# Products of the identity with itself in TensorE's waits between the last ranks and the first layer's first product

## The chip, the cores and the metric

The kernel runs on one core of one Trainium2 chip. The time is device microseconds from one launch; "before" is the median of three runs. One more execution was profiled, and all views of engines, waits and clock come from that execution. The engines are TensorE (PE; its weight loads are PEld), VectorE (DVE), ScalarE (ACT), GpSimd (POOL) and SyncE (SP, which here only issues DMAs). "Granted clock" is the share of TensorE's full clock that the throttle let through.

## The reference

4096 tokens of 512 numbers are rotated by a quaternion product, routed to two of eight experts each with a capacity of 1024 slots per expert, passed through the expert's two layers, weighted and added to the input.

```python
def reference(x, cond_256, q_right, spectral_gate, gate_w, fc1_w, fc1_b, fc2_w, fc2_b):
    xr = hamilton(normalize(cond_256), hamilton(x * spectral_gate, conj(normalize(q_right))))
    xf = xr.reshape(4096, 512)
    scores = softmax(xf @ gate_w.T)                  # 8 experts
    topv, topi = top_k(scores, 2)
    gates = topv / topv.sum(-1, keepdims=True)
    # place of each (token, choice) in its expert: all first choices, then all second choices
    loc = running_count_per_expert(topi)             # valid while loc < 1024
    de = scatter(xf, topi * 1024 + loc)              # (8, 1024, 512)
    h = relu(de @ fc1_w.T + fc1_b)                   # (8, 1024, 2048)
    eo = h @ fc2_w + fc2_b                           # (8, 1024, 512)
    return x + sum_over_choices(eo[slot] * gates * valid)
```

The filter in the reference (a transform, a gain for each channel, the inverse transform) is a gain for each channel. Everything is f32.

## The kernel before, in words

The kernel has two parts. The first is the routing, inside a block that ends at line 535. The 4096 tokens are taken in two groups of 16 tiles of 128 tokens (`GROUPS`, `last` is 1). For each group `logits` (line 328) multiplies the tokens by the rotated gate, `turned` and `choose` find the two experts on VectorE and build running counts `cnt`, `rank` (line 387) sums the counts over the partitions on TensorE, and `places` turns ranks into a tile number and a lane for each token's slot. `one_hots` (lines 428 to 433) builds f16 arrays W and A on VectorE for half a group (8 tiles of tokens, 16 pairs of token and choice). `tokens` (line 444) is 16 products of A's and W's slices, 128x64 each, that add up in one PSUM bank `tok_ps`: after four calls the bank holds which token sits in which slot.

The order in which the engines get their instructions is the order of the program text (`manual_schedule`), each engine taking its own in turn. Around the change it is: ranks of the last group, one_hots and tokens of the first group's second half (0,1), a few tensor operations on POOL that find which slots are taken, places and then one_hots and tokens of the last group's halves (last,0) and (last,1); the A of the very last half is built in two parts of eight pairs (`parts=2`). VectorE then makes `slot_tok`, `tokf` and `slot_add` (lines 501 to 506); four f32 products (line 510) spread tokf into `quarter_ps`, which line 525 turns into the gather indices `quarter` of later experts; lines 529 to 535 make `slot_cho`.

`lt_ps` are the two PSUM banks of the logits, read for the last time by `turned`. `ident` is a 128x128 f32 identity, made by POOL near the start and used for transposes.

The second part is the experts. `first_layers` begins by gathering the first expert's eight rows of 128 slots from x (POOL, line 560, indices slot_tok), and `rotated(0)` transposes the first four rows on TensorE (line 687, four 128x128 transposes a row, one for each quarter j, into four banks `xps`), then applies the rotation: ScalarE writes the j = 0 share of output quarter i (line 695), VectorE adds j = 1, 2, 3 (line 697). The result is `xa`. Four f32 products for each i (line 833 in `layer1_plain`, tile `p`, two blocks and two halves m; eight MATMUL instructions) make the first quarter of the first expert's first layer. `rotated(1)` does the same for the other four rows (tiles `xc`, `xb`) after three of the four i groups have been issued. From the second quarter on, layers run in the seven-product form (`layer1`, line 722, and the second layers, line 735), for 8 experts of 4 quarters each, and a generator pair interleaves first and second layers on TensorE. POOL computes sums of blocks for them (lines 124 to 139) and gathers the next expert's rows (`xq`, line 637).

PSUM after line 535 is divided into `ps_x` (one bank), `ps_1` (two buffers of two banks, tag p1: the first layer's accumulators) and `ps_2` (three banks). Buffers of a tag are handed out in turn.

Of the kernel before, what the change touches and what calls it, by code (L numbers as in the profile page):

```python
# [28 lines left out]
F32 = mybir.dt.float32  # L29
# [8 lines left out]
P = 128  # L38
# [9 lines left out]
HALF = 512  # L48
PER = HALF // P
# [15 lines left out]
def kernel(  # L65
# [12 lines left out]
    nc = tc.nc  # L78
# [16 lines left out]
    ident = const.tile([P, P], F32, name="ident")  # L95
# [4 lines left out]
    slot_add = const.tile([P, NS], I32, name="slot_add")  # L100
    slot_cho = const.tile([P, NS], I32, name="slot_cho")
    quarter = const.tile([P, NS, QT], I32, name="quarter")

    def load_w1(k):
        e, g = divmod(k, NG)
        w = wpool.tile([P, 2, 2, 2, HB], F32, tag="w1", name=f"w1_{k}")
        nc.sync.dma_start(w, w1[e, g])
        return w

    def load_w2(k):  # L110
        e, g = divmod(k, NG)
        w = wpool.tile([P, 2, 2, D], F32, tag="w2", name=f"w2_{k}")
        nc.sync.dma_start(
            w, w2[e, g * HG : (g + 1) * HG, :].rearrange("(a c p) d -> p a c d", p=P, c=2)
        )
        return w
# [14 lines left out]
    def left1(k, w):  # L131

        s = [wsum.tile([P, 2, HB], F32, tag=f"s{i}", name=f"s{i}_{k}") for i in range(4)]
        G = nc.gpsimd
        steps = [
            lambda: G.tensor_tensor(s[0], w[:, 1, 0], w[:, 1, 1], ALU.add),  # L136
            lambda: G.tensor_tensor(s[1], s[0], w[:, 0, 0], ALU.subtract),
            lambda: G.tensor_tensor(s[2], w[:, 0, 0], w[:, 1, 0], ALU.subtract),
            lambda: G.tensor_tensor(s[3], w[:, 0, 1], s[1], ALU.subtract),  # L139
        ]  # L140
        return [w[:, 0, 0], w[:, 0, 1], s[3], w[:, 1, 1], s[0], s[1], s[2]], steps

    def right2(k, w):

        return sums(
            wsum,
            "t",
            k,
            [P, 2, DB],
            w[:, 0, :, :DB],  # L150
            w[:, 0, :, DB:],
            w[:, 1, :, :DB],
            w[:, 1, :, DB:],
            minus=True,
        )
# [10 lines left out]
    with ExitStack() as rctx:  # L166
# [8 lines left out]
        def bank(pool, tag, n=""):  # L175
            return pool.tile([P, 512], F32, tag=tag, name=f"{tag}{n}")
# [145 lines left out]
        lt_ps = [bank(rps, "lt", g) for g in range(GROUPS)]  # L322
# [95 lines left out]
        def one_hots(g, c, hi, lo, parts=1):  # L418

            hi, lo = (  # L420
                a[:, c * TC : (c + 1) * TC].rearrange("p t k -> p (t k)") for a in (hi, lo)
            )
            tok = tok_no[:, g * TG + c * TC : g * TG + (c + 1) * TC].rearrange("p t k -> p (t k)")
            of_tile = [P, NS, TC * K]
            B = oh.tile(of_tile, F16, tag="B", name=f"B{g}_{c}")
            W[g, c] = oh.tile(of_tile, F16, tag="W", name=f"W{g}_{c}")
            A[g, c] = oh.tile([P, P, TC * K], F16, tag="A", name=f"A{g}_{c}")
            V.tensor_tensor(B, tile_no, hi.unsqueeze(1).to_broadcast(of_tile), ALU.is_equal)
            V.tensor_tensor(W[g, c], B, tok.unsqueeze(1).to_broadcast(of_tile), ALU.mult)
            n = TC * K // parts  # L430
            for i in range(parts):
                part = slice(i * n, (i + 1) * n)
                V.tensor_tensor(
                    A[g, c][:, :, part],
                    lane[:, :, part],
                    lo[:, part].unsqueeze(1).to_broadcast([P, P, n]),
                    ALU.is_equal,
                )

        def tokens(g, c):  # L440

            for t in range(TC):
                for k in range(K):
                    nc.tensor.matmul(  # L444
                        tok_ps[:, k, :],
                        lhsT=A[g, c][:, :, t * K + k],
                        rhs=W[g, c][:, :, t * K + k],
                        start=g == 0 and c == 0 and t == 0 and k == 0,
                        stop=g == GROUPS - 1 and c == TG // TC - 1 and t == TC - 1,
                        skip_group_check=True,  # L450
                    )
# [16 lines left out]
        rank(last)  # L468
        one_hots(0, 1, *at)
        tokens(0, 1)  # L470


        SE = [P, E, PT]
# [18 lines left out]
        at = places(last)  # L492
        one_hots(last, 0, *at)
        tokens(last, 0)
        one_hots(last, 1, *at, parts=2)
        tokens(last, 1)


        has0, not0, any_ = (a.rearrange("p e s -> p (e s)") for a in (has0, not0, any_))
# [9 lines left out]
        for c in range(QT):  # L509
            nc.tensor.matmul(  # L510
                quarter_ps[:, c],
                lhsT=spread[:, c].rearrange("p q w -> p (q w)"),
                rhs=tokf,
                start=True,
                stop=True,
            )


        den = rp.tile([P, NT], F32, name="den")
# [8 lines left out]
        t = rp.tile([P, NS], F32, name="t")  # L528
# [20 lines left out]
    ps_1 = ctx.enter_context(tc.tile_pool(name="ps_1", bufs=2, space=PSUM))  # L549
# [304 lines left out]
    def first_layers():  # L854

        xs = Slots(0)
        xs.gather(0)
        xs.gather(1)
        load_b2(0)

        def rotated(half):

            t = [xs.bank(half, j, *((ps_x, "xps") if j == 3 else (ps_2, "p2"))) for j in range(NJ)]
            for st in range(PER):
                for j in range(NJ):
                    xs.transpose(half, j, st, t[j])
            for i in range(NJ):
                for j in range(NJ):
                    xs.add(half, i, j, t[j])

        rotated(0)
        xf, fill = xs.factors()
        left_f, w1_t, w2_t = None, None, None
        nxt = None
        for k in range(NK):
            e, g = divmod(k, NG)
            if k + 1 < NK:
                w1_t, w2_t = load_w1(k + 1), load_w2(k + 1)
                left_n, steps = left1(k + 1, w1_t)
                loaded[k + 1] = w2_t  # L880
            else:
                left_n, steps = None, []
            if g == 0 and e + 1 < E:
                nxt = Slots(e + 1)
            if g == NG - 1 and e + 1 < E:
                xf_n, fill_n = nxt.factors()
                steps = [f for pair in zip(steps, fill_n) for f in pair]
                per = 2
            else:
                per = 1  # L890
            if k == 0:
                rights[0], more = right2(0, w2_next)
                for f in [*more, *steps]:
                    f()
                steps = []
            units = layer1(k, (left_f, xf)) if k else layer1_plain(k, w1_next, xs)
            for i, _ in enumerate(units):
                if k == 0 and i == 2:
                    rotated(1)
                    for f in fill:  # L900
                        f()
                if k == 0 and i == 1:
                    nc.scalar.dma_start(choice.rearrange("(p t) c -> p t c", p=P), picked)

                    nc.scalar.dma_start(*(a.rearrange("(b r) d -> r b d", r=PT) for a in (out, x)))
                if e + 1 < E:

                    if (g, i) in ((0, 12 if e else 5), (1, 6)):
                        fetches.extend(nxt.quarters(g))
                    if (g, i) in ((1, 9), (2, 5)):  # L910
                        background.extend(nxt.steps(g - 1))

                if i in (7, 8, 9, 13):
                    assert per == 1 or nxt.rotated == 2 * NJ
                    for f in steps[:per]:
                        f()
                    steps = steps[per:]
                yield
            left_f = left_n
            if g == NG - 1 and e + 1 < E:  # L920
                xf = xf_n
# [6 lines left out]
    def load_b2(e):  # L928
        b2_sb = op.tile([P, D], F32, tag="b2", name=f"b2_{e}")
        nc.gpsimd.dma_start(b2_sb, b2[e : e + 1, :].to_broadcast([P, D]))  # L930
        biases[e] = b2_sb.unsqueeze(1).to_broadcast([P, 4, D])
# [138 lines left out]
```

## Time and profile before

| what | us |
|---|---|
| runs before: lowest, median, highest | 1649.4, 1653.91, 1654.48 |
| the profiled execution, its time | 1635.26 |
| its span, first to last instruction | 1633.5 |
| mean granted clock of TensorE over the span | 0.988 |
| TensorE's wait for the logits' weights, at the start | 6.2 |
| TensorE's waits for VectorE's A (three) | 5.7 |
| TensorE's waits for the first expert's rows (three) | 2.6 |
| TensorE's wait for xa ahead of the first layer's first product | 2.7 |

The table's waits are TensorE's idle time ahead of an instruction, by what released it. A block in the timeline stands as start, length, engine, line, operation, output and inputs, shape and count; its length runs from the first start to the last modelled end, so the last instruction's pass through the array is in it. A window row gives each engine's busy time in that stretch and, after them, the granted clock. The first eight MATMULs of the logits take 1.94 us, the fifth such block 1.59 us and the sixth 1.06 us; in the trace the granted clock reads 1.00 until its first recorded change.

### The profile page before, as it was taken

The page shows a single profiled execution, that of the slowest core. Times are in us where ns is not written, and L with a number is a line of the kernel's source. Part 1 is how long each engine was busy: PE and PEld are TensorE (multiplying, and loading weights), DVE is VectorE, ACT ScalarE, POOL GpSimd, SP SyncE. Part 2 cuts the span into 40 slices and gives each one's busy share as a digit, 9 for nine tenths or more (in the row PEclk, how much of TensorE's full clock was granted, in tenths as well). Part 3 has the DMA queues.
Part 4 walks back from the last instruction along what each step waited for, and adds up shares of the span by engine and source line. Part 5 has one row for each costly group of instructions (what it writes and reads, how often), then busy time and mean ns, then how long its engine had stood idle before and what let it go on. Part 6 is the DMA issues. An engine that isn't in the chain of part 4 may idle for free.

```text
span 1633.5 us, 14524 instructions
## 1 busy us (share of the span) xinstructions
PE 1582.3 (97%) x5558; PEld 1039.0 (64%) x5558; DVE 912.3 (56%) x1291; ACT 284.5 (17%) x393; POOL 897.0 (55%) x747
## 2 busy tenths in 40 slices
PE   4899999999999999999999999999999999999996
PEld 1456666666666666666666666666666666666665
DVE  7537744575455754577345774457644575454335
ACT  1122111221112211122111211121111221111110
POOL 1576255862668445784367735586266844544304
PEclk8799999999999999999999999999999999999999
DMA  7542103311222113320133210331122311230003
GB/s 311 176 147 72 52 5 139 110 64 52 96 75 92 54 52 110 116 74 17 52 127 114 75 52 1 140 112 66 52 81 72 105 55 52 104 108 30 23 26 102
DMA packets 47998, 137.31 MB, mean 84 GB/s; under 512 B 9334, under 2 KB 9590, under 8 KB 42808
## 3 DMA queue, kind: packets, MB, share of 16 engines
q1 hardware_dynamic: 22800, 75.54, 12.5%
q0 software_dynamic: 20736, 52.32, 9.7%
q10 hardware_dynamic: 4392, 8.52, 1.4%
q8 instruction: 44, 0.72, 0.2%
q14 instruction: 26, 0.21, 0.0%
HBM read 119.77 MB, written 25.23 MB: 89 GB/s over the span
## 4 chain that ended last, share of the span: by engine, by line
PE 91%; DVE 2%; issue 2%; ACT 2%; DMA 2%; POOL 1%; SPq 0%; POOLq 0%; DVEq 0%; ACTq 0%
PE a L735 26%; PE a L722 25%; PE b L722 20%; PE b L735 18%; PE p L833 2%; ACT xa L695 1%; DMA xb<-in_xt_dram 1%; DVE xps L652 1%; DMA rows<-out_dram,slot_tok 0%; POOL rows L560 0%; POOL out_dram L606 0%; ACT u L766 0%; PE tok_ps L444 0%; ACT h L766 0%; DMA rows<-in_x_dram,slot_tok 0%
## 5 line engine op out<-in xcount | busy, mean ns | idle before, releaser
L766 ACT ACTIVATE u<-a,b_sb 128x512 f32<-128x512 f32 x186 | 127.9, 687 | 851.7 <-PE a L722 851.7
L637 POOL DMA_INDIRECT xq<-in_xq_dram,quarter x224 | 231.2, 1032 | 62.0 <-issue 58.4
L735 PEld LDWEIGHTS a<-t,hs 128*128 128x128 f32 x1024 | 194.6, 190 | 79.4 <-issue 59.3
L735 PE MATMUL a<-t,hs 128*128 128x256 f32 x1024 | 241.9, 379 | 0.0
L722 PE MATMUL a<-x,s 128*128 128x512 f32 x496 | 233.1, 592 | 0.0
L136 POOL TENSOR_TENSOR s<-w 128x512 f32<-128x512 f32 x31 | 39.3, 1268 | 224.2 <-PE b L722 224.1
L139 POOL TENSOR_TENSOR s<-w,s 128x512 f32<-128x512 f32 x31 | 39.7, 1279 | 204.1 <-PE b L722 204.0
L722 PEld LDWEIGHTS a<-x,s 128*128 128x128 f32 x496 | 94.2, 190 | 65.7 <-issue 59.3
L722 PE MATMUL a<-x,w 128*128 128x512 f32 x248 | 117.3, 595 | 9.7 <-ACT h L766 9.7
L735 PEld LDWEIGHTS b<-w,h 128*128 128x128 f32 x512 | 97.2, 190 | 42.1 <-issue 20.6
L735 PE MATMUL b<-w,h 128*128 128x256 f32 x512 | 121.1, 379 | 2.1 <-DVE acc L996 2.1
L735 PEld LDWEIGHTS a<-t,h 128*128 128x128 f32 x512 | 97.1, 190 | 40.5 <-issue 25.1
L735 PEld LDWEIGHTS a<-w,h 128*128 128x128 f32 x512 | 97.3, 190 | 39.7 <-issue 29.7
L735 PEld LDWEIGHTS b<-t,hs 128*128 128x128 f32 x512 | 97.3, 190 | 39.7 <-issue 26.5
L735 PEld LDWEIGHTS b<-w,hs 128*128 128x128 f32 x512 | 97.3, 190 | 39.3 <-issue 28.9
L735 PE MATMUL a<-t,h 128*128 128x256 f32 x512 | 121.1, 379 | 0.8 <-DVE v L983 0.8
L735 PE MATMUL b<-t,hs 128*128 128x256 f32 x512 | 121.0, 379 | 0.0
L735 PE MATMUL a<-w,h 128*128 128x256 f32 x512 | 121.0, 379 | 0.0
L735 PE MATMUL b<-w,hs 128*128 128x256 f32 x512 | 120.9, 379 | 0.0
L722 PE MATMUL a<-xa,w 128*128 128x512 f32 x248 | 116.6, 592 | 0.8 <-ACT u L766 0.8
L722 PE MATMUL b<-xa,w 128*128 128x512 f32 x248 | 116.5, 592 | 0.0
L722 PE MATMUL b<-x,s 128*128 128x512 f32 x248 | 116.5, 592 | 0.0
(169 smaller groups left out, 2143.3 us busy)
## 6 DMA issues: line engine op xcount, KB each, us to landing
w<-in_w_dram SPq DMA_DIRECT2D x64, 1024.0 KB, 7.8
xb<-in_xt_dram SPq DMA_DIRECT2D x8, 1024.0 KB, 11.2
out_dram<-in_x_dram ACTq DMA_DIRECT2D x1, 8192.0 KB
xq<-in_xq_dram,quarter POOLq DMA_INDIRECT x224, 2.5
b<-in_b_dram POOLq DMA_DIRECT2D x8, 256.0 KB, 3.6
c<-choice,slot_cho POOLq DMA_INDIRECT x64, 3.1
rows<-out_dram,slot_tok POOLq DMA_INDIRECT x64, 5.8
out_dram<-rows,slot_add POOLq DMA_INDIRECT x64, 2.8
```

The source lines that it names most:

```text
L136: lambda: G.tensor_tensor(s[0], w[:, 1, 0], w[:, 1, 1], ALU.add),
L139: lambda: G.tensor_tensor(s[3], w[:, 0, 1], s[1], ALU.subtract),
L637: nc.gpsimd.indirect_dma_start(out=self.xg[half][st][:, q * P : (q + 1) * P], out_offset=None, in_=xq, in_offset=bass.IndirectOffsetOnAxis ...
L652: V.transpose(t[:, st * P : (st + 1) * P].rearrange("p (q w) -> p q w", w=CW), self.xg[half][st].rearrange("p (q j w) -> p j q w", q=QT, j ...
L695: nc.scalar.activation(to, t, AF.Copy, scale=M[:, i, 0:1])
L722: nc.tensor.matmul(out[:, m], lhsT=factors[0][n][:, c, m * P : (m + 1) * P], rhs=factors[1][n][:, c, :], start=first and c == 0, stop=c == ...
L735: nc.tensor.matmul(out[:, m], lhsT=factors[0][n][:, c, (st0 + m) * P : (st0 + m + 1) * P], rhs=factors[1][n][:, c, :], start=first and m = ...
L766: nc.scalar.activation(to[:, m], a[:, m], func, bias=bias[:, m : m + 1])
L833: nc.tensor.matmul(ps[n][:, m], lhsT=w[:, block, i // 2, i % 2, m * P : (m + 1) * P], rhs=x.of(half, i), start=i == 0, stop=i == NJ - 1,)
```

## The change

A helper `idle(t, n)` issues n products of `ident` with `ident` into the first 128 columns of a PSUM tile; nobody reads the result. It is called with 5 after tokens(0,1), 5 after tokens(last,0), 6 after tokens(last,1) and 10 after the line 510 products, all into `lt_ps[0]`. In `rotated(0)` it is called with 3 after each of the first three rows' transposes and 12 after the fourth, into a `spare` tile that is taken from `ps_1` (tag p1) ahead of the first layer's own tiles. That is 47 products. `rotated(1)` has none.

```diff
+    def idle(t, n):
+
+        for _ in range(n):
+            nc.tensor.matmul(t[:, :P], lhsT=ident, rhs=ident, start=True, stop=True)
@@
         one_hots(0, 1, *at)
         tokens(0, 1)
+        idle(lt_ps[0], 5)
@@
         one_hots(last, 0, *at)
         tokens(last, 0)
+        idle(lt_ps[0], 5)
         one_hots(last, 1, *at, parts=2)
         tokens(last, 1)
+        idle(lt_ps[0], 6)
@@
                 start=True,
                 stop=True,
             )
+
+        idle(lt_ps[0], 10)
@@
             t = [xs.bank(half, j, *((ps_x, "xps") if j == 3 else (ps_2, "p2"))) for j in range(NJ)]
+            spare = ps_1.tile([P, 2, HALF], F32, tag="p1", name="spare")[:, 0] if half == 0 else None
             for st in range(PER):
                 for j in range(NJ):
                     xs.transpose(half, j, st, t[j])
+                if half == 0:
+                    idle(spare, 3 if st + 1 < PER else 12)
```

## The prediction

> **What bounds the kernel now.** I read the page first, for the engine that sets the span and for the clock granted to it.
>
> ```profile
> span 1633.5 us, 14524 instructions
> PE 1582.3 (97%) x5558; PEld 1039.0 (64%) x5558; DVE 912.3 (56%) x1291; ACT 284.5 (17%) x393; POOL 897.0 (55%) x747
> PEclk8799999999999999999999999999999999999999
> ```
>
> The reader sees TensorE busy 97% of the span and a granted clock that is down only in the first slices (40.8 us each). All the change touches lies there, so I read the chain of waits over the first 120 us (start, length, what).
>
> ```profile
> 38.03 1.15 DVE A L433
> ...
> 39.23 4.21 PE tok_ps L444 x32
> ...
> 44.44 1.25 POOL rows L560
> ...
> 47.26 3.92 DMA rows<-in_x_dram,slot_tok
> ...
> 51.23 1.34 PE xps L687 x5
> ...
> 52.64 0.70 ACT xa L695
> ...
> 55.89 13.49 PE p L833 x24
> 69.38 1.75 PE xps L687 x16
> 71.12 17.34 PE p L833 x40
> ```
>
> The chain runs through the last tokens products, the POOL row gathers, the third row's landing, transposes, ScalarE and VectorE (three adds of 0.76 us), and from 55.89 TensorE itself. The same p products cost 17.34/40 = 0.434 us at the end and 13.49/24 = 0.562 us at the start: 24 at 0.434 would be 10.40, so 3.09 us are lost. Then TensorE's timeline, with the idle time before each block in brackets, shows where fills can go.
>
> ```profile
> 26.75 2.22 PE L444 MATMUL tok_ps<-W,A 128*128 128x64 f16 x16 [1.87 <-DVE A L433]
> 35.12 2.19 PE L444 MATMUL tok_ps<-W,A 128*128 128x64 f16 x16 [1.93 <-DVE A L433]
> 39.23 4.20 PE L444 MATMUL tok_ps<-W,A 128*128 128x64 f16 x32 [1.91 <-DVE A L433]
> 44.43 1.94 PE L510 MATMUL rank<-tokf,spread 128*128 128x64 f32 x8 [1.00 <-DVE tokf L505]
> 51.23 1.97 PE L687 MATMUL xps<-ident,rows 128*128 128x128 f32 x8 [0.48 <-DMA rows<-in_x_dram,slot_tok]
> 69.21 1.91 PE L687 MATMUL xps<-ident,rows 128*128 128x128 f32 x16
> ```
>
> Last, busy time by 2 us windows (length, then PE, PEld, DVE, ACT and POOL busy with instruction counts, granted clock, DMA share, GB/s) dates the clock.
>
> ```profile
> 26.00:28.00 2.00, 1.25 (x10) 1.26 (x11) 1.90 (x5) 0.01 (x1) 0.00 (x0) 0.92 1.07 399
> 28.00:30.00 2.00, 0.96 (x8) 0.80 (x7) 1.73 (x6) 0.31 (x1) 0.00 (x0) 0.50 1.03 419
> 60.00:62.00 2.00, 2.00 (x4) 0.76 (x3) 1.93 (x4) 0.00 (x0) 1.92 (x3) 0.55 0.43 108
> 62.00:64.00 2.00, 2.00 (x6) 0.87 (x5) 0.53 (x1) 0.00 (x0) 2.00 (x3) 1.00 0.52 199
> ```
>
> The clock falls to half in the first row (0.92 is full for 84%: at 27.7) and rises in the third (0.55: 10%, at 61.8), 5.9 us after the p products began. Half of 5.9 is 2.95, which explains the 3.09 lost.
>
> **The change part by part.** Nothing is removed or moved. Added are 47 full f32 products of ident with itself, all on TensorE: 5, 5, 6, 10, three times 3, and 12. No DMA is issued, and no engine reads their banks in this stretch. The spare tile swaps which p1 buffer the first layer uses first; line 525, the last VectorE reader of the banks under the two buffers, ends at 47.1, before 55.89, so no wait is added by it.
>
> Price of one. A full f32 product is two instructions (line 510's four products are eight). The nearest instruction of that size is the f32 transpose of line 687: at half clock eight take 1.97 with the last 0.42 long, spaced (1.97-0.42)/7 = 0.22; at full clock sixteen take 1.91, the last 0.27, spaced 0.109. So one costs 0.44 at half clock and 0.22 at full: the two bounds. The tokens products are 4.20-2.19 over 16 = 0.126 apart, and the block at 26.75, which spans the clock's fall, takes the same 2.22: they gain nothing from a faster clock.
>
> A, five after tokens(0,1). The last token issues at 37.31-0.31 = 37.00, the fills start at 37.13 and end at half clock by 39.33, against 39.23 when A lets the next tokens go: +0.1. Behind them wait only tokens products.
>
> B, five between tokens(last,0) and tokens(last,1). The 32 tokens run as one block with no wait inside it: sixteen issue by 39.23+2.02 = 41.25, and the first half of the next A ends about 41.1. So there is nothing to fill and all of it is on the chain: 1.1 at full clock, 2.2 at half. Everything up to the row gathers is late by that.
>
> C, six before the quarter products. Between the last token's issue (43.13+0.13) and 44.43 lie 1.17 us; the fills take 1.32 at full clock, so the quarter products are 0.15 late. Who waits is VectorE's line 525 and the choice slots, which hold slack until line 697 at 53.36: nothing.
>
> D, ten before the first transpose. The quarter products then take 8 x 0.109 = 0.9 instead of 1.94 and end near 45.5; ten add 2.2, to 47.7, and the first row is there at 48.17 (all plus B's delay): hidden.
>
> E, three after each of the first three rows' transposes. A row takes 4 x 0.109 + 0.66 = 1.1 at full clock; rows come at 48.17, 49.63 and 51.23, so two are hidden. After the third, its transposes end about 51.7 and the fills at 52.4, where the fourth row's first transpose used to end at 52.57: +0.2 at most for ScalarE.
>
> F, twelve after the fourth row: 2.64, between about 52.9 and 55.5, before VectorE frees the first product at 55.89: hidden.
>
> What it buys: the 3.09 us, if the clock is up by 55.89. VectorE doesn't take over: it adds an i group in 3 x 0.76 = 2.3 us, and eight p instructions take 3.44. Later waits (POOL's xq gathers, about 112 to 120) hang on POOL's sums, which waited 2.1 us for VectorE's xb adds and those for the second transposes, so they move with TensorE.
>
> When does the clock rise? TensorE is occupied without a break from 35.12 with the fills. In the trace the rise took 5.9 us of dense products. Whether tokens count as such is open: the clock fell at 27.7 while some ran, after sparse work. If they count, the rise comes by 41.3 and B costs 1.1: 0.1+1.1+0.2-3.09 = -1.7. If not, B runs at half and the rise comes in C or D, since fills, quarter products and fills again make 8 us in a row: 0.1+2.2+0.2-3.09 = -0.6. I take the middle, -1.2 (profiled time 1635.26 to 1634.1), and keep both ends.
>
> A rule to weigh: the Trainium skill, "TensorE: Matmul & The Clock Gate", Part 1, says that the clock rises after one busy window of about 3.4 us that runs free of the kernel, and that the ramp is under 1% of a typical span and differs from run to run. By it the wait for the clock lies between 3.4 and 6.8 us, this trace's 5.9 is near its long end, and a mean execution would lose, by an estimate from that page, some 2.5 instead of 3.09; the sum would then be -1.1 to 0.0.
>
> The three runs before have a median of 1653.91, 18.65 above the profiled time; I carry that unchanged: 1653.91-1.2 = 1652.7.
>
> **The rivals.**
>
> *Faster* (0.18). The timed executions are 18.65 us longer than the profiled one, and no view says where. If in them the clock rose only after all 24 first products, each eight would take 16 x 0.434 = 6.9 instead of 3.47: 10.4 us lost, and the change would give 1.4-10.4 = -9.0, 1645. For it: the gap, and the 5 us spread of three runs. Against: dense products raised the clock within 5.9 us here.
>
> *Slower* (0.11): the fills don't raise the clock, and pace the rows at half rate. Its place is the stretch from C to F. From the last token's issue, 43.26+2.3 (A and B): C 2.64, quarter products 1.76, D 4.4, so the first transposes start at 54.4 instead of 48.2; three rows of 0.88+1.32 bring 61.0, the fourth row 0.88 and F 5.28 bring 67.1 where the p products started at 55.89: +11.2, and the 3.09 stays lost: 1665. It decides if D runs wholly at half clock. For it: tokens kept TensorE busy for all 2 us from 40 to 42, and tokens and quarter products for 1.42 and 1.57 us of the next two windows, and the clock stayed at half. Against: from C on no gap is left, and gapless work at 56 to 62 did raise it.
>
> *It does what it says and nothing comes of it* (0.06): the second expert's gathers at 112 to 120 are held by the DMA traffic and not by TensorE, and swallow the gain: then 1653.9 to 1655. Against it is the releaser of POOL's sums above.
>
> **How the numbers follow.** My forecast has 0.65. What a measurement of this kernel can tell from no change is about 0.3%, 5.0 us. Forecast and third rival lie within it but for the scatter of medians (three runs spread over 5.08 us), which I put at 0.04 beyond on the fast side and 0.02 on the slow side: faster 0.18+0.04 = 0.22, slower 0.11+0.02 = 0.13, same 0.65. The forecast's own range is -1.7 to -0.6 with half that spread on either side, 1649.7 to 1655.8. To hold 8 in 10 it reaches part of the way to both outer cases: 1646 to 1659.5.
>
> **What would show it.** Right: fills of 0.22 us each from some point between 38 and 48 us, a granted clock of 1.00 in the windows from there on, the tok_ps block split with 1.1 to 2.2 us of fills inside, the first p products some 1.4 to 2.5 us later than 55.89, and 24 of them in about 10.4 us. Wrong on C to F: transposes starting more than 0.5 us after a row's landing, or a p start later than 59. Wrong on the gain: 24 products still over 12 us, a fall of the clock after its rise, or a gain in the first 90 us that is gone by 130 us.

## The result, and the profile after

The changed kernel took 1655.8 us (median of 22 runs, 1652.25 to 1662.01), beside 1651.34 for the kernel before in 22 runs of its own. The ratio is 1.0031, 95% interval 1.0022 to 1.0040: some 5 us slower (3.6 to 6.6). 1.2 us faster was predicted. The page of the changed kernel's profiled execution (1655.6 us):

```profile
span 1653.8 us, 14710 instructions
PE 1602.1 (97%) x5652; PEld 1053.9 (64%) x5652; DVE 912.0 (55%) x1291; ACT 284.3 (17%) x393; POOL 896.4 (54%) x747
PEclk6899999999999999999999999999999999999999
```

The 47 products are 94 more MATMULs (5652 - 5558). The chain of waits, from the last A on (start, length, what; "another core or an unknown queue" stands for a wait whose releaser the profile does not find):

```profile
41.50 16.73 another core or an unknown queue x2
58.24 0.00 issue
58.24 0.70 ACT xa L705
...
61.49 12.26 PE p L843 x24
73.75 1.75 PE xps L697 x16
75.50 17.34 PE p L843 x40
92.84 1.73 PE a L732 x4
```

Before, ScalarE's first xa began at 52.64, 0.50 us after the fourth row's first transpose (52.14). Now it begins at 58.24, and the profile cannot name what released it: between the semaphore's last wait and that moment it finds no TensorE instruction that ended then. TensorE's timeline shows when the transposes were sent off:

```profile
39.05 2.17 PE L449 MATMUL tok_ps<-W,A 128*128 128x64 f16 x16
41.04 2.41 PE L107 MATMUL lt<-ident 128*128 128x128 f32 x10
43.24 2.18 PE L449 MATMUL tok_ps<-W,A 128*128 128x64 f16 x16
...
48.95 2.45 PE L107 MATMUL lt<-ident 128*128 128x128 f32 x20
51.23 0.61 PE L697 MATMUL xps<-ident,rows 128*128 128x128 f32 x4
...
54.56 0.60 PE L697 MATMUL xps<-ident,rows 128*128 128x128 f32 x4
55.00 1.39 PE L107 MATMUL spare<-ident 128*128 128x128 f32 x11
56.56 0.50 PE L107 MATMUL spare<-ident 128*128 128x128 f32 x3 [0.17 <-issue]
57.31 0.27 PE L107 MATMUL spare<-ident 128*128 128x128 f32 x1 [0.25 <-issue]
58.02 1.27 PE L107 MATMUL spare<-ident 128*128 128x128 f32 x9 [0.44 <-issue]
61.49 12.26 PE L843 MATMUL p<-xa,w 128*128 128x512 f32 x24 [2.20 <-DVE xa L707]
```

Two things are to be seen. The five products between the token halves stand as a bare block, 41.04 to 43.24. And the fourth row's transposes are recorded at 54.56, yet ScalarE starts 3.68 us later, while the fills behind them stutter with pauses that nothing in the profile ends. A product that another engine waits for raises a semaphore, a counter that the engines share, and the trace has the times of these updates. Those of the fourth row's four transposes, whose modelled ends are 54.84 to 55.16, are recorded at 58.17 to 58.27, some 0.03 us apart, closer than such transposes are recorded to run (0.109 each). The last transposes of the second and third row are late too (modelled 52.95 and 54.06, updated 55.84 and 58.06). In the kernel before, every update in this stretch follows its modelled end within 0.02 us. So a modelled end need not be the completion. The row itself was not late: the last DMA packet of its gather ended at 54.12, before the transposes were recorded.

Busy time by windows (length; PE, PEld, DVE, ACT, POOL busy with counts; granted clock; DMA share; GB/s) shows the clock:

```profile
48.00:50.00 2.00, 2.00 (x18) 2.00 (x17) 0.82 (x3) 0.00 (x0) 1.70 (x2) 0.91 0.63 164
...
60.00:62.00 2.00, 0.51 (x1) 0.30 (x2) 1.90 (x3) 0.66 (x2) 2.00 (x2) 1.00 0.42 114
62.00:64.00 2.00, 2.00 (x4) 0.94 (x3) 1.93 (x4) 0.00 (x0) 1.92 (x3) 0.51 0.52 188
64.00:66.00 2.00, 2.00 (x4) 0.72 (x4) 1.93 (x4) 0.00 (x0) 2.00 (x3) 0.64 0.53 205
```

The clock did rise ahead of the p products, at 48.4. But since these were late, TensorE was idle from 59.3 to 61.5, and the clock fell again at 62.0 for 3.4 us, inside the very products it was raised for: 24 of them took 12.26 instead of 10.40.

### The profile page after: what moved, and what is told of

Read it like the earlier page. It is cut to its first block, busy times and chain, and to the rows that moved or that the text cites. A ratio compares the mean times of both kernels' runs of the same rounds, so it can differ in the third digit from the quotient of the medians.

```text
span 1653.8 us, 14710 instructions
## 1 busy us (share of the span) xinstructions
PE 1602.1 (97%) x5652; PEld 1053.9 (64%) x5652; DVE 912.0 (55%) x1291; ACT 284.3 (17%) x393; POOL 896.4 (54%) x747
## 3 DMA queue, kind: packets, MB, share of 16 engines
q10 hardware_dynamic: 4392, 8.52, 1.3%
## 4 chain that ended last, share of the span: by engine, by line
PE 91%; ACT 2%; issue 2%; DVE 2%; POOL 1%; DMA 1%; another core or an unknown queue 1%; SPq 0%; POOLq 0%; DVEq 0%; ACTq 0%
PE a L745 26%; PE a L732 26%; PE b L732 19%; PE b L745 18%; PE p L843 2%; ACT xa L705 1%; DMA xb<-in_xt_dram 1%; POOL rows L570 0%; ACT h L806 0%; POOL out_dram L616 0%; ACT u L776 0%; DVE A L438 0%; ACT h L776 0%; DMA rows<-out_dram,slot_tok 0%
## 5 line engine op out<-in xcount | busy, mean ns | idle before, releaser
L647 POOL DMA_INDIRECT xq<-in_xq_dram,quarter x224 | 226.9, 1013 | 62.2 <-issue 60.6
L732 PE MATMUL a<-x,w 128*128 128x512 f32 x248 | 122.0, 616 | 17.2 <-ACT h L776 13.8
L732 PEld LDWEIGHTS a<-x,s 128*128 128x128 f32 x496 | 94.2, 190 | 65.7 <-issue 59.3
```

The lines of the kernel that those rows point to most:

```text
L647: nc.gpsimd.indirect_dma_start(out=self.xg[half][st][:, q * P : (q + 1) * P], out_offset=None, in_=xq, in_offset=bass.IndirectOffsetOnAxis ...
L732: nc.tensor.matmul(out[:, m], lhsT=factors[0][n][:, c, m * P : (m + 1) * P], rhs=factors[1][n][:, c, :], start=first and c == 0, stop=c == ...
```

## The experiments

One measure runs through all of them: stages on TensorE's side from the start of tokens(last,0), which makes small shifts of the beginning fall out. Each column is the time from the point before it: "gathers" from that start to POOL's first gather, "fourth row" from there to that row's first transpose, "ScalarE" to the first xa, "p" to the first p product, "to layer" to the first product of the seven-product layers (line 722 of the kernel before), then the sum of all. The stages come from one profiled execution, the ratio from 9 to 22 executions beside 22 to 35 of the kernel before; 0.001 is 1.65 us, and the two differ by up to 2.5 us.

| kernel | gathers | fourth row | ScalarE | p | to layer | sum | ratio to before, 95% |
|---|---|---|---|---|---|---|---|
| before | 5.21 | 7.70 | 0.51 | 3.25 | 32.42 | 49.1 | 1 |
| b_again (before) | 5.22 | 7.72 | 0.56 | 3.25 | 32.11 | 48.9 | |
| after | 7.38 | 8.13 | 3.68 | 3.25 | 31.19 | 53.6 | 1.0031 (1.0022 to 1.0040) |
| after_again | 6.31 | 7.84 | 3.80 | 3.25 | 31.19 | 52.4 | 1.0035 (1.0021 to 1.0048) |
| no_b | 5.20 | 10.22 | 1.52 | 3.24 | 29.49 | 49.7 | 1.0009 (0.9999 to 1.0018) |
| b_only | 7.41 | 7.69 | 0.56 | 3.25 | 32.01 | 50.9 | 1.0006 (0.9996 to 1.0016) |
| routing_only | 7.40 | 7.73 | 0.41 | 3.25 | 31.19 | 50.0 | 1.0012 (1.0001 to 1.0023) |
| rotated_only | 5.22 | 8.77 | 2.63 | 3.24 | 30.90 | 50.8 | 1.0001 (0.9993 to 1.0010) |
| short_w1 | 5.22 | 8.66 | 2.15 | 3.26 | 29.49 | 48.8 | 1.0011 (0.9997 to 1.0025) |
| wide256 | 5.21 | 8.52 | 0.36 | 3.74 | 29.50 | 47.3 | 1.0001 (0.9989 to 1.0014) |
| rotated_wide | 5.20 | 9.36 | 0.36 | 3.25 | 29.49 | 47.7 | 0.9985 (0.9976 to 0.9995) |
| twelve_only | 5.20 | 7.76 | 0.56 | 4.05 | 29.39 | 47.0 | 0.9988 (0.9975 to 1.0002) |
| after_wide | 6.26 | 7.76 | 0.41 | 3.25 | 29.49 | 47.2 | 0.9998 (0.9988 to 1.0009) |
| fitted | 5.20 | 7.84 | 0.41 | 3.25 | 29.49 | 46.2 | 0.9982 (0.9973 to 0.9990) |

**b_again.** No edit: what is the kernel before like in another execution?

> The kernel before, unchanged, profiled once more. The profiled execution of before took 1635.26 us, its timed executions 1648 to 1655. Theory A (that execution was an odd one): this one takes 1648 to 1655, the first layer's products start within 0.5 us of 55.9, and the extra 15 us lie in longer waits of TensorE for ScalarE and in half-clock windows at the six later expert boundaries, as in the profile of the changed kernel (4 half-clock windows, 13.8 + 4.3 us of waits there). Theory B (the changed kernel causes those): about 1635 us, no half-clock window after 62 us, waits of 9.7 + 0.8 us.

It took 1646.94 us, 1 us under the range of theory A, and p started at 55.30, 0.6 from 55.9. TensorE's waits (us in total, times, longest), first of the first profile of before:

```profile
PE a L722 <- ACT h L766: 9.7, 7, 1.5
...
PE a L722 <- ACT u L766: 0.8, 1, 0.8
```

Then of b_again, with a window at a later expert boundary:

```profile
PE a L722 <- ACT h L766: 13.8, 7, 2.2
...
PE a L722 <- ACT u L766: 2.6, 7, 0.8
...
712.00:714.00 2.00, 2.00 (x4) 0.86 (x3) 1.97 (x5) 0.00 (x0) 1.70 (x2) 0.64 0.11 33
```

Theory A holds in the main: the boundary waits of 13.8 us are there without the change, and so are half-clock windows (three, each 3.41 us). The first profiled execution of before had 9.7 and 0.8 us of these waits and no such window. By an estimate from these figures that is 5.9 us of waits and half of 10.2 us, 11.0 of the 11.7 us between the two executions; the rest up to the median isn't accounted for. Setting the two first profiles side by side would have charged the change with all of it; up to the seven-product layers, the profiles of before agree to 0.2 us.

**no_b, b_only, routing_only, rotated_only.** The parts, each by leaving out calls of `idle`:

```diff
# no_b: the changed kernel without
-        idle(lt_ps[0], 5)            # after tokens(last, 0)
# b_only: the kernel before with that call alone
# routing_only: the changed kernel without
-                if half == 0:
-                    idle(spare, 3 if st + 1 < PER else 12)
# rotated_only: these alone
```

> The changed kernel without the five products between tokens(last,0) and tokens(last,1). Theory 1 (these five lie bare on the chain): the tokens block ends 2.0 us earlier than in the changed kernel, near 43.5, and the time is some 2 us less: +3 us (ratio 1.0015 to 1.002) against before. Theory 2 (the loss is in the late transposes' completion): 0 to 1 us less, ratio 1.0025 to 1.003. Theory 3 (they are what raises the clock early): the clock rises a window later and the time stays or grows: 1.003 to 1.004.

> The kernel before with only the five products between tokens(last,0) and tokens(last,1). Theory 1 (they lie bare on the chain): the last tokens product and the gathers come 2.1 us later, nothing else changes, ratio 1.0010 to 1.0015. Rival (something hides them, or VectorE's A sets that time): ratio 1.0000 to 1.0005.

> The changed kernel without the products between the rows' transposes (3, 3, 3 and 12); the 26 products of the routing stay. Theory 1 (the loss is the five bare products, the rest hidden): +2 us before the gathers stays, the clock falls or not, ratio 1.001 to 1.0015. Theory 2 (dense products among the transposes hold their completion back by some 3 us, so ScalarE starts at 58.2 instead of 55): ScalarE starts its first xa within 0.3 us of the last row's first transpose, the first p product near 58.2 and not 61.5; ratio 1.0000 to 1.0015, at least 2 us under the changed kernel.

> The changed kernel with only the products between the rows' transposes (3, 3, 3 and 12); none in the routing. Theory 1: nothing is late before the gathers; at half clock the three fills of 1.3 us pace the rows a little (up to +1.5 us), the twelve raise the clock before or during the first p products (-1.5 to -3 us): ratio 0.999 to 1.000. Theory 2 (these products hold the transposes' completion back): ScalarE's first xa starts 2 us or more after the fourth row's first transpose; ratio 1.001 to 1.002.

The bare block is what it looked like. TensorE's timeline of b_only:

```profile
39.29 2.19 PE L449 MATMUL tok_ps<-W,A 128*128 128x64 f16 x16 [1.90 <-DVE A L438]
41.30 2.42 PE L107 MATMUL lt<-ident 128*128 128x128 f32 x10
43.51 2.18 PE L449 MATMUL tok_ps<-W,A 128*128 128x64 f16 x16
```

The second half starts 2.2 us later than it would back to back, the gathers 2.2 us later (7.41 against 5.21), and nothing else in the row of the table moves. Its ratio is worth 1 us, and the interval, -0.7 to 2.6 us, holds the 2.2 and also the rival's 0 to 0.8: here the stages decide, not the time. In no_b the gathers are on time again, and its ratio, 1.0009, is clear of the changed kernel's, though below the range of all three theories. Its fourth row is 2.5 us late: the six fills, the quarter products and the first of the ten fills (the clock rose at 49.6) ran at half clock, and then TensorE waited 0.94 us for a completion of its own ahead of the first row's last transpose.

The hold-up appears only where short fills stand among the transposes: ScalarE starts 1.5 to 3.8 us after the fourth row's first transpose in after, after_again, no_b and rotated_only, and 0.4 to 0.6 in routing_only, b_only and before. So rotated_only wins nothing in time although nothing of it lies ahead of the gathers (its ratio, 1.0001, lies between the ranges of its two theories), and routing_only, without these fills, is some 3 us under the changed kernel, as theory 2 has it.

**rotated_wide, after_wide.** Is it TensorE's time that the fills take, or their number? The same columns in few products:

```diff
+    def idle(t, n, src):
+        cols = n * P
+        while cols:
+            c = min(cols, 512)
+            nc.tensor.matmul(t[:, :c], lhsT=ident, rhs=src[:, :c], start=True, stop=True)
+            cols -= c
...
+                    idle(spare, 3 if st + 1 < PER else 12, w1_next[:, 0, 0].rearrange("p a b -> p (a b)"))
```

In the routing, src is the 512 columns of `spread`.

> As rotated_only, but the columns of the fills are taken in few wide products (one of 384 columns after each of the first three rows, three of 512 after the fourth, of ident with a slice of the first w1 tile): the same array time, 2 to 6 instructions in place of 6 to 24. Theory 2a (many short instructions in a row hold the completions back): ScalarE's first xa starts within 0.6 us of the fourth row's first transpose (rotated_only: 2.6), the 24 p products take under 11 us, ratio 0.9985 to 0.9995. Theory 2b (TensorE's occupied time itself does it, the transposes stand behind the fills): the lag of 1.5 us or more stays, ratio 1.000 to 1.001.

> The changed kernel with every fill in wide products of the same columns in all (512 at most in one). Theory 2a: what is left of the loss is the bare five (+2 us at half clock) and the pacing, the gain of the early clock comes through: ScalarE starts within 0.6 us of the fourth row's first transpose, ratio 0.9995 to 1.0010. Theory 2b: ratio 1.002 to 1.004 as the changed kernel.

TensorE and ScalarE around the fourth row, first of rotated_only, then of rotated_wide:

```profile
52.96 0.60 PE L692 MATMUL xps<-ident,rows 128*128 128x128 f32 x4
53.40 2.84 PE L107 MATMUL spare<-ident 128*128 128x128 f32 x24
58.83 4.67 PE L838 MATMUL p<-xa,w 128*128 128x512 f32 x7 [2.59 <-DVE xa L702]
...
55.59 0.69 ACT L700 ACTIVATE xa<-xps,M 128x512 f32<-128x512 f32 x1 [22.88 <-remote]
```

```profile
53.67 0.60 PE L695 MATMUL xps<-ident,rows 128*128 128x128 f32 x4
54.11 2.74 PE L109 MATMUL spare<-w,ident 128*128 128x512 f32 x6
57.28 6.28 PE L841 MATMUL p<-xa,w 128*128 128x512 f32 x14 [0.43 <-DVE xa L705]
...
54.03 0.69 ACT L703 ACTIVATE xa<-xps,M 128x512 f32<-128x512 f32 x1 [21.17 <-issue]
```

TensorE's recorded time for the last fills is the same, 2.84 and 2.74 us; 24 MATMULs, each with its weight load, have become 6, and ScalarE starts 0.36 us after the transpose instead of 2.63. TensorE's idle time before p falls from 2.59 to 0.43, and the clock doesn't fall again. Both kernels come out as theory 2a says, and after_wide, all the change's columns with the bare block among them, is 5 to 6 us under the changed kernel and level with the kernel before. Whether the number of MATMULs does it or that of the weight loads, which fell with them, no run here tells.

**after_again, short_w1, wide256, twelve_only.** Does it repeat, and what of the short fills does it?

> The changed kernel, unchanged, beside the variants on one chip. If the hold-up among the short fills is a property of the kernel and not of one execution, ScalarE's first xa again starts 2 to 4 us after the fourth row's first transpose, and the ratio is 1.002 to 1.004; if it was one odd execution, the start comes within 0.6 us and the ratio near 1.000 to 1.001.

> As rotated_only, 21 short fills of 128 columns, but with a slice of the first w1 tile as the moving operand in place of ident itself. Theory 2a (the number of short instructions): ScalarE's first xa again starts 1.5 to 4 us after the fourth row's first transpose, ratio 1.000 to 1.001. Theory 2c (ident is read from one place as both operands): within 0.6 us, ratio 0.9985 to 0.9995.

> As rotated_wide, with at most 256 columns in one product: 384 as 256 + 128 after each of the first three rows, six of 256 after the fourth. By theory 2a the hold-up depends on how many instructions come in a microsecond: with half the number it should be small, ScalarE's start 0.4 to 1.0 us after the fourth row's first transpose, ratio 0.9985 to 0.9998. If 256 columns are still too short: 1.5 us or more, ratio 1.000.

> As rotated_only, with the twelve short fills after the fourth row alone, so that no transpose stands behind a fill. If the hold-up comes from the short fills in the queue ahead of the transposes: ScalarE starts within 0.6 us of the fourth row's first transpose, and the ratio is 0.999 to 1.000 (part of the clock's rise is won). If short fills behind hold completions back as well: 1 us or more, ratio 1.000 to 1.001.

short_w1 changes `rhs=ident` to `rhs=src[:, :P]` with the w1 slice, wide256 changes 512 to 256 in the wide helper, twelve_only makes the condition `half == 0 and st + 1 == PER`. It repeats, 3.80 us at a ratio of 1.0035, though there the clock was up at 41.5: an earlier clock doesn't help. With another moving operand the hold-up stays (2.15; its ratio, 1.0011, is just over the range expected), so theory 2c falls. With half the number of MATMULs (wide256) the hold-up shrinks but is still there: ScalarE is in time (0.36), as the row's first transpose is, but the semaphore's updates of the other three come at 54.80 to 54.87, about 1 us after their modelled ends (53.70 to 53.92). VectorE, which needs them, starts 0.5 us late, and the ratio is 1.0001 where 0.9998 or less was expected. With the twelve alone, behind all transposes, ScalarE starts as in the kernel before; they still ran at half clock at first and made p 0.8 us late, and the ratio can't be told from 1 nor from rotated_wide. So fills behind the last transposes, at half clock as they were here, did not hold these up; fills among the rows did. The hold-up does not simply go by the number of short fills ahead of the row: with 30 of them (no_b) ScalarE starts 11.7 us after the first gather, with 9 (rotated_only) 11.4, where the kernel before has 8.2.

**fitted.** Wide fills cut to the gaps at half clock, and none where there is no gap: 512 columns after tokens(0,1), 256 after tokens(last,1), 512 after the line 510 products, 128 after each of three rows, and three times 512 after the fourth.

> Wide fills cut to the gaps at half clock: 512 columns after tokens(0,1), none between the last two token halves, 256 after tokens(last,1), 512 after the line 510 products, 128 after each of the first three rows, three of 512 after the fourth. Theory 2a: nothing is delayed and the clock is up before the first p product: p starts as before, 24 of them take 10.4 us, ratio 0.998 to 0.999. Theory 2b: transposes' completion late by 1 us or more, ratio 0.9995 to 1.0005.

```profile
52.11 0.66 PE L699 MATMUL xps<-ident,rows 128*128 128x128 f32 x4 [0.60 <-DMA rows<-in_x_dram,slot_tok]
52.60 2.74 PE L109 MATMUL spare<-w,ident 128*128 128x512 f32 x6
55.77 7.56 PE L845 MATMUL p<-xa,w 128*128 128x512 f32 x17 [0.43 <-DVE xa L709]
```

The p products start 16.7 us after tokens(last,0), as before, and all at full clock. Every stage of the table is the kernel before's but the last, which is 2.6 to 2.9 us shorter. The ratio, 0.9982 (0.9973 to 0.9990), is the lowest of all, 3 us under the kernel before and clear of both kernels, though not of rotated_wide and twelve_only.

## Why the prediction was wrong

The price of a product, A and the clock's rise were right: ten MATMULs take 2.41 with the last one's tail, and the clock was up at 48.4 and, in after_again, at 41.5, where some point between 38 and 48 was forecast.

B was right in both bounds: 2.2 us at half clock (7.38 - 5.21), 1.1 at full (6.31 - 5.21 in after_again, 1.05 in after_wide).

C and D cost 0.1 to 0.4 at the fourth row, where nothing was forecast: in the profiled execution C's fills and part of the quarter products still ran at half clock, so D's fills began at 48.95 only and ended at 51.40, after the first row's last packet (49.81).

E is the step that failed: "+0.2 at most for ScalarE". It measured 3.2 to 3.3 (3.68 and 3.80 against 0.51). I had taken the spacing at which TensorE's records follow each other (0.109) for the rate at which work completes. The row it came from is sixteen transposes with no fills among them, and there it holds: ScalarE starts 0.31 us after the thirteenth, the last row's first. With short fills among the rows the records keep that spacing, and the updates of the second to fourth row come 2.9 to 4.0 us after the modelled ends. The cause behind that stays open.

"What it buys" failed as a consequence: 1.23 of 3.09 came, as F's twelve fills ended 2.2 us before the late p products, and the clock fell. Summed from the table, 2.17 + 0.43 + 3.17 - 1.23 = +4.5 for after and 1.10 + 0.14 + 3.29 - 1.23 = +3.3 for after_again; the medians differ by 4.5 and 5.1. So the parts account for the loss within 2 us, no better than the stages of single executions agree with the ratios elsewhere in the table.

The slower rival had the place, C to F, and a start of p later than 59 as its sign, but not the mechanism: it had the clock stay at half. The faster rival rested on the 18.65 us between profile and runs; b_again shows 11.7 of them, at the expert boundaries, not here.

## What to carry to other kernels

Work that only keeps TensorE's clock up should be wide (512 columns here; 256 were not enough), not many short products among those that others wait for, and belongs where TensorE waits, never between two blocks that run back to back. What matters about a short instruction ahead of a consumer is when its completion is seen, so read the consumer's start and not the producer's modelled end. Before comparing two profiles, profile the old kernel twice.

## What the runs showed of the hardware

Here short f32 products among transposes at full clock held back the completion of these, by up to 3.3 us at the consumer; by what mechanism stays open. It isn't the columns that pass (rotated_wide), the operand (short_w1) or a late row (the fourth row's last packets ended at 54.12 in the changed kernel and at 51.79 in rotated_only, before its transposes). Not every run of short products does it: in routing_only and after_again the quarter products stand right behind six fills at full clock, and their semaphore update comes 0.01 us after the modelled end. The timed executions were all recorded by the profiler, so whether recording each instruction takes part in it wasn't tried.

The tokens products are 0.126 us apart at half clock (before) and 0.124 at full (after_again, after_wide). And the clock can fall on short pauses: 2.2 us of idle time before p in the changed kernel, or a window from 710 to 712 us in b_again in which TensorE was busy for 0.39 of 2.00 us, each came just before 3.41 us at half clock. The Trainium skill, "TensorE: Matmul & The Clock Gate", section "Why this matters for your kernels", asks for no idle gaps over about 3 us between bursts of products. Here gaps of about 2 us were sometimes enough. Their length alone doesn't decide, for in short_w1 the granted clock stayed at 1.00 through 2.13 us of idle time:

```profile
57.44 7.13 PE L838 MATMUL p<-xa,w 128*128 128x512 f32 x16 [2.13 <-DVE xa L702]
```
